# Two attention layers in float32 on one core: projections by seven half-size products, and group-norm averages on VectorE

## The chip, the cores and the metric

The kernel runs on one core of one Trainium2 chip. The metric is the device time of one execution in microseconds; before the change the median of three runs is 4166.9 us (4165.38 to 4168.29).

## The reference, cut to what matters

The input x has 8 images of 32 x 32 positions and 512 channels. Two layers follow each other, each a group norm (32 groups of 16 channels), three projections, attention, and an output projection added onto x:

```
qkv = gn(x) @ w_qkv                          # layer 0: 16 heads of 32
x = x + softmax(q k^T / sqrt(32)) v @ w_proj + b_proj
q, k, v = gn(x) @ Wq, gn(x) @ Wk, gn(x) @ Wv # layer 1: 4 heads of 128
x = x + softmax((q k^T + position logits) / ..) v @ Wo
```

All of it is float32. Per image there are eight products of [1024 x 512] by [512 x 512]: q, k, v and the output projection of each layer.

## The kernel before, in words

Everything is held transposed, channels on partitions: a `block` is [128, 4 chunks, 1024 positions], and eight blocks are in SBUF at a time. PSUM has eight banks: four for the logits of attention 0 (`ps`, one buffer), one for its accumulator (`acc`, one buffer), and three (`bank`) that all else takes in turn.

**Projections.** `project_T` (L210) and `product_T` (L468) make an output [128 channels x 512 positions] in one bank as the sum over four chunks; `project_rows` (L228) makes v with positions on partitions. Each [128 x 128] weight is used as four column tiles of 32 by `by_columns` (L202, matmul at L206). A float32 matmul shows as two instructions in the trace, so one bank is 32 instructions: 4 chunks x 4 column tiles x 2. A projection is 8 banks. `evacuate` (L128, L130) copies a bank to SBUF on ScalarE; the output projections add it onto x on VectorE (L490, L525). Weights come whole, 1 MB, by `load_weight` (L132) on SyncE's queue, two buffers deep.

**Attention 0** (L272) goes by steps of 128 keys. `front` computes logits for 512 queries of four heads (L282) and exponentials on ScalarE (L290, 2048 columns). `back` multiplies by v (L301) and adds up the exponentials on VectorE (`esum`, L310 and L312). After eight steps `hold` copies the accumulator (L262) and `finish` sums `esum` over partitions by matmuls (L321) and calls `normalise` (L265): reciprocal on VectorE (L268), a check of the sums (L249), and a multiplication on GpSimd (L270). **Attention 1** (L382) does the same with 512 columns a step and with the position logits of `position_logits` (L344), whose copies from PSUM alternate between ScalarE (L377) and VectorE (L378).

**Group norm.** `statistics` (L164) takes mean and variance of each channel; `group_norm` (L172) averages over 16 channels by two small matmuls with `gavg` (L176, L186) and normalises in place (L192).

**The order of the work.** The main loop runs b from 0 to 8. In round b the 64 steps of attention 0 of image b go side by side with a list of other work: `after_0` of image b-1 (output projection of layer 0), `after_1` of image b-2 (that of layer 1) with `norm_1` of image b-1 between its parts, `second` of image b-1 (q, k, v of layer 1 with position logits), attention 1 of image b-1 with `load` of image b+1 woven in, and `before_0` of image b+1 (q, k, v of layer 0). `side_by_side` (L548) spreads that list over the steps by the costs that each part yields, one unit being one chunk's matmuls. Attention 1 yields 0, so its 64 steps run together between two steps of attention 0. In round 1 there is no `after_1`, and `norm_1` gets empty cost of 3 x 8 (`ALONE`) in its place:

```
            if past is not None:
                rest.append(woven(after_1(b - 2, past), norm, 1, 1))
                total += PRODUCT
            else:
                rest.append(chain([ALONE], (cost + ALONE for cost in norm)))
                total += 3 * ALONE
```

The tile framework then makes the order on each engine: an instruction that its own plan finds ready may be put ahead of earlier ones that wait. At run time each engine takes its instructions strictly in that order.

Of the kernel before, what the change touches and what calls it, by code (L numbers as in the profile page):

```python
# [9 lines left out]
F32 = mybir.dt.float32  # L10
# [17 lines left out]
def quick_path(  # L28
# [40 lines left out]
    small = ctx.enter_context(tc.tile_pool(name="small", bufs=4))  # L69
# [20 lines left out]
    with nc.allow_non_contiguous_dma(reason="512 values, once"):  # L90
# [6 lines left out]

    ng = P // GROUP_CHANNELS
    gind = consts.tile([P, ng], F32, tag="gind", name="gind")
    nc.vector.tensor_reduce(  # L100
        gind, ident.rearrange("p (g k) -> p g k", k=GROUP_CHANNELS), axis=AX.X, op=ALU.add
    )
    gavg = consts.tile([P, P], F32, tag="gavg", name="gavg")
    nc.vector.tensor_scalar(
        gavg.rearrange("p (g k) -> p g k", k=GROUP_CHANNELS),
        gind.unsqueeze(2).to_broadcast([P, ng, GROUP_CHANNELS]),
        1.0 / GROUP_CHANNELS,
        None,
        op0=ALU.mult,
    )  # L110
# [17 lines left out]
    def evacuate(dst, src):  # L128

        nc.scalar.copy(dst, src)  # L130

    def load_weight(w, col0, name):  # L132
        t = mem.tile([P, CC, NB], F32, tag="w", name=name, bufs=2)
        nc.sync.dma_start(t, w.rearrange("(cc p) n -> p cc n", p=P)[:, :, col0 : col0 + NB])
        return t
# [9 lines left out]
    def fetch(kept, name):  # L145
        xT = chunks(block(name))
        for cc in range(CC):
            nc.sync.dma_start(xT[cc], kept[cc])
        return xT
# [5 lines left out]
    def load_blocks(b, cc):  # L155

        xs = mem.tile([P, N // 32, 32], F32, tag="xs", name=f"xs_{b}_{cc}", bufs=2)
        for a in range(P // 32):
            nc.sync.dma_start(
                xs[32 * a : 32 * a + 32], by_blocks(xf[b], cc * P + 32 * a)  # L160
            )
        return xs.rearrange("p t i -> p (t i)")

    def statistics(st, xT, cc, name):  # L164
        if cc == 0:
            st["mv"] = small.tile([P, CC, 2], F32, tag="mv", name=f"mv_{name}")
        s = small.tile([P, NH, 6], F32, tag="st", name=f"st_{name}_{cc}")
        for h in range(NH):
            nc.vector.bn_stats(s[:, h, :], xT[cc][:, h * NB : (h + 1) * NB])
        nc.vector.bn_aggr(st["mv"][:, cc, :], s.rearrange("p h s -> p (h s)"))  # L170

    def group_norm(st, xT, name):  # L172

        mv = st["mv"]
        pm = bank(f"pm_{name}", [P, CC])
        nc.tensor.matmul(pm, gavg, mv[:, :, 0], start=True, stop=True)  # L176
        mean = small.tile([P, CC], F32, tag="mean", name=f"mean_{name}")
        nc.vector.tensor_copy(mean, pm)

        off = small.tile([P, CC], F32, tag="off", name=f"off_{name}")  # L180
        nc.vector.tensor_sub(off, mv[:, :, 0], mean)
        nc.vector.tensor_mul(off, off, off)
        nc.vector.tensor_add(off, off, mv[:, :, 1])
        yield 0
        pv = bank(f"pv_{name}", [P, CC])
        nc.tensor.matmul(pv, gavg, off, start=True, stop=True)  # L186
        var = small.tile([P, CC], F32, tag="var", name=f"var_{name}")
        nc.vector.tensor_scalar_add(var, pv, GN_EPS)
        rstd = small.tile([P, CC], F32, tag="rstd", name=f"rstd_{name}")
        nc.gpsimd.tensor_tensor(rstd, var, neg_half, op=ALU.pow)  # L190
        for cc in range(CC):
# [10 lines left out]
    def by_columns(out, weights, moving, start, stop):  # L202

        for g in range(P // 32):
            columns = slice(32 * g, 32 * g + 32)
            nc.tensor.matmul(  # L206
                out[columns, :], weights[:, columns], moving, start=start, stop=stop
            )

    def project_T(xn, w, dsts, name):  # L210

        for m in range(CC):
            for h in range(NH):
                pa = bank(f"pa_{name}_{m}_{h}")
                for cc in range(CC):
                    by_columns(
                        pa,
                        w[:, cc, m * P : (m + 1) * P],
                        xn[cc][:, h * NB : (h + 1) * NB],
                        start=(cc == 0),  # L220
                        stop=(cc == CC - 1),
                    )
                    if cc == CC // 2 - 1:
                        yield CC // 2
                evacuate(dsts(m)[:, h * NB : (h + 1) * NB], pa)
                yield CC // 2

    def project_rows(xn, w, y, name):  # L228

        for t in range(NT):  # L230
            pa = bank(f"pa_{name}_{t}")
            for cc in range(CC):
                by_columns(
                    pa,
                    xn[cc][:, t * P : (t + 1) * P],
                    w[:, cc, :],
                    start=(cc == 0),
                    stop=(cc == CC - 1),
                )
                if cc == CC // 2 - 1:  # L240
                    yield CC // 2
            evacuate(y[:, t, :], pa)
            yield CC // 2

    def check_sums(rec, su, name):
        junk = mem.tile([P, NB], F32, tag="junk", name=f"jk_{name}", bufs=1)
# [3 lines left out]
            out=junk,  # L250
# [8 lines left out]

    def hold(acc, name):  # L260
        held = mem.tile([P, NB], F32, tag="held", name=f"hd_{name}", bufs=2)
# [837 lines left out]
```

## Time and profile before

| | |
|---|---|
| median of three runs | 4166.9 us |
| the profiled execution | 4168.86 us |
| its span, first to last instruction | 4167.1 us |
| mean granted TensorE clock | 0.995 |
| busy: TensorE, VectorE, ScalarE, GpSimd | 4068.1, 2295.5, 1663.9, 279.7 us |
| TensorE on the eight projections (L206) | 234 to 243 us each over the 8 images |
| DMA | 172.10 MB, mean 41 GB/s |

In the profile PE is TensorE's matmuls, PEld its weight loads, DVE VectorE, ACT ScalarE, POOL GpSimd and SP the queue of SyncE. A line of a group reads: line, engine, operation, output<-inputs, shapes, count | busy us, mean ns of one | idle us before them and what ended it. The end of a matmul is modelled, and matmuls overlap, so the time between the starts of matmuls says more than a mean duration does.

### The profile page before, as it was taken

Reading aid. Unit: us, or ns where it says so; the run is one execution under the profiler, and the core shown is the slowest. Engines: PE = TensorE matmul, PEld = TensorE weight load, DVE = VectorE, ACT = ScalarE, POOL = GpSimd, SP = SyncE. Lnnn points to the kernel's source line nnn. Section 1 sums busy time; section 2 is a strip of 40 time slices with the busy share of each in tenths; the row PEclk is TensorE's granted clock in tenths of the full one; section 3 lists DMA queues with packets and bytes.
Section 4 is the critical chain, followed back from the end, with each engine's and each line's share of the span. In section 5 each row is a group of like instructions: output and inputs, shape, how many; then the busy total and the mean of one; then the engine's idle time right before and its main releaser. Section 6 shows DMA issues by size and latency. Waiting matters only on the chain.

```text
span 4167.1 us, 64679 instructions
## 1 busy us (share of the span) xinstructions
PE 4068.1 (98%) x28866; PEld 1359.1 (33%) x28866; DVE 2295.5 (55%) x1977; ACT 1663.9 (40%) x1665; POOL 279.7 (7%) x155
## 2 busy tenths in 40 slices
PE   7999999999999999999999999999999999999998
PEld 2222234222442224322243223432234322234343
DVE  2566565464654655546555564655556457555244
ACT  1554543434434343343533435344453444542131
POOL 0000000000010000100000000000000000001000
PEclk9999999999999999999999999999999999999999
DMA  4101020031200302012020120202210022010201
GB/s 122 31 31 41 11 61 0 21 97 37 51 1 24 109 21 51 1 68 65 21 51 11 67 57 21 51 11 72 52 37 25 11 77 46 15 57 2 70 31 22
DMA packets 320896, 172.10 MB, mean 41 GB/s; under 512 B 271424, under 2 KB 271456, under 8 KB 320608
## 3 DMA queue, kind: packets, MB, share of 16 engines
q1 hardware_dynamic: 320512, 167.81, 14.2%
q8 instruction: 228, 3.74, 0.4%
q14 instruction: 60, 0.49, 0.0%
q0 software_dynamic: 96, 0.07, 0.0%
HBM read 117.51 MB, written 50.33 MB: 40 GB/s over the span
## 4 chain that ended last, share of the span: by engine, by line
PE 90%; DVE 6%; ACT 3%; DMA 0%; issue 0%; SPq 0%; POOL 0%; DVEq 0%; ACTq 0%; POOLq 0%
PE ps L282 12%; PE acc L301 11%; PE ps L392 10%; PE pa_q L206 10%; PE pp L206 10%; PE acc L404 10%; PE pa_k L206 9%; PE pa_v L206 9%; PE ps L393 3%; DVE rc L268 2%; ACT e L290 2%; PE su L321 1%; ACT posT L377 1%; PE su L423 1%; DVE es L310 1%; DVE posT L378 1%
## 5 line engine op out<-in xcount | busy, mean ns | idle before, releaser
L290 ACT ACTIVATE e<-ps 128x2048 f32<-128x2048 f32 x512 | 961.5, 1878 | 955.7 <-PE ps L282 789.0
L312 DVE TENSOR_TENSOR es<-es,e 128x2048 f32<-128x2048 f32 x384 | 880.1, 2292 | 701.4 <-ACT e L290 701.4
L282 PE MATMUL ps<-q,k 32*128 32x512 f32 x4096 | 605.9, 644 | 47.5 <-ACT e L290 47.4
L268 DVE RECIPROCAL rc<-su 128x512 f32<-128x512 f32 x128 | 429.8, 3357 | 358.6 <-PE su L321 326.7
L395 ACT ACTIVATE e<-ps 128x512 f32<-128x512 f32 x512 | 305.9, 597 | 709.9 <-PE ps L393 656.9
L301 PE MATMUL acc<-e,v 128*32 128x512 f32 x4096 | 550.4, 610 | 1.0 <-ACT e L290 1.0
L392 PE MATMUL ps<-q,k 128*128 128x512 f32 x1024 | 534.5, 604 | 5.5 <-ACT e L395 5.5
L404 PE MATMUL acc<-e,v 128*128 128x512 f32 x1024 | 522.3, 593 | 0.0
L270 POOL TENSOR_TENSOR q<-hd,rc 128x512 f32<-128x512 f32 x128 | 259.4, 2027 | 3617.9 <-DVE rc L268 3165.6
L415 DVE TENSOR_TENSOR es<-es,e 128x512 f32<-128x512 f32 x384 | 285.8, 744 | 252.1 <-ACT e L395 250.9
L393 PE MATMUL ps<-posT,sel 128*128 128x512 f32 x512 | 406.9, 795 | 0.0
L282 PEld LDWEIGHTS ps<-q,k 32*128 32x128 f32 x4096 | 165.3, 183 | 479.2 <-issue 256.7
L392 PEld LDWEIGHTS ps<-q,k 128*128 128x128 f32 x1024 | 184.3, 189 | 268.7 <-issue 185.2
L206 PE MATMUL pa_v<-wv,x1T 128*32 128x512 f32 x2048 | 243.4, 594 | 0.0
L206 PE MATMUL pa_k<-x1T,wk 128*32 128x512 f32 x2048 | 242.5, 596 | 0.0
L206 PE MATMUL pa_q<-x0T,wq 128*32 128x512 f32 x2048 | 238.0, 599 | 3.5 <-DVE x0T L192 3.5
L404 PEld LDWEIGHTS acc<-e,v 128*128 128x128 f32 x1024 | 192.6, 189 | 145.3 <-issue 103.8
L206 PE MATMUL pp<-q,wo 128*32 128x512 f32 x2048 | 235.6, 592 | 2.9 <-DVE checks L249 2.9
L206 PE MATMUL pa_q<-x1T,wq 128*32 128x512 f32 x2048 | 236.6, 594 | 0.0
L206 PE MATMUL pa_v<-wv,x0T 128*32 128x512 f32 x2048 | 235.8, 592 | 0.0
L206 PE MATMUL pa_k<-x0T,wk 128*32 128x512 f32 x2048 | 235.8, 592 | 0.0
L206 PE MATMUL pp<-q,wp 128*32 128x512 f32 x2048 | 234.4, 592 | 0.0
(67 smaller groups left out, 2276.7 us busy)
## 6 DMA issues: line engine op xcount, KB each, us to landing
xs<-in_x SPq DMA_DIRECT2D x128, 128.0 KB, 3.4
d<-x0T SPq DMA_DIRECT2D x32, 512.0 KB, 3.8
x1T<-d SPq DMA_DIRECT2D x32, 512.0 KB, 5.7
d<-x1T SPq DMA_DIRECT2D x32, 512.0 KB, 2.6
x2T<-d SPq DMA_DIRECT2D x32, 512.0 KB, 7.9
out<-ot SPq DMA_DIRECT2D x256, 64.0 KB, 1.9
wq<-in_L_conv_w_qkv SPq DMA_DIRECT2D x8, 1024.0 KB, 5.2
wk<-in_L_conv_w_qkv SPq DMA_DIRECT2D x8, 1024.0 KB, 5.6
```

The source lines that it names most:

```text
L206: nc.tensor.matmul(out[columns, :], weights[:, columns], moving, start=start, stop=stop)
L268: nc.vector.reciprocal(rec, su)
L270: nc.gpsimd.tensor_tensor(dst, held, rec, op=ALU.mult)
L282: nc.tensor.matmul(ps[:, r, :], k[m][rows, j * P : (j + 1) * P], q[m][rows, h * NB : (h + 1) * NB], start=True, stop=True,)
L290: nc.scalar.activation(e, ps, AF.Exp, scale=D0 ** -0.5)
L301: nc.tensor.matmul(acc[r * D0 : (r + 1) * D0, :], v[:, j, c0 : c0 + D0], e[:, r, :], start=(j == 0), stop=(j == NT - 1),)
L312: nc.vector.tensor_add(state["esum"], state["esum"], e)
L392: nc.tensor.matmul(ps, k[h][:, keys], q[:, h, queries], start=True, stop=False)
L393: nc.tensor.matmul(ps, sel[:, keys], posT[:, h, queries], start=False, stop=True)
L395: nc.scalar.activation(e, ps, AF.Exp, scale=1.0 / math.sqrt(D1))
L404: nc.tensor.matmul(acc, v[:, j, h * D1 : (h + 1) * D1], e, start=(j == 0), stop=(j == NT - 1),)
L415: nc.vector.tensor_add(state["esum"], state["esum"], e)
```

## The change

**Seven products.** The products go by the Winograd form of Strassen's method. The input is cut into halves of channels (two chunks each, `HC`) and of positions (`NB` = 512), the weight into halves of both sides. `forms` makes three sums of quarters of the input in buffers of their own and one in place, four VectorE instructions of 1024 columns. Four sums of quarters of each weight are made once, at the start (`add_up`), and kept in DRAM: for w_qkv on VectorE, for the other five weights on GpSimd and its queue.

`seven` makes a quarter of an output pair, two units `u` a projection. It has three banks x, y and z, and seven products in the order 0, 5, 6, 4, 1, 2, 3, each of two chunks:

```
        x = bank(f"x_{name}")
        product(x, 0, True)
        p1 = snapshot("e1", f"p1_{name}")
        nc.scalar.copy(p1, x)
        yield HC
        y = bank(f"y_{name}")
        product(y, 5, True)
        a = snapshot("es1", f"a_{name}")
        nc.vector.tensor_add(a, y, p1)
        sink.early(p1, a)
        yield HC
        z = bank(f"z_{name}")
        product(z, 6, True)
        p7 = snapshot("e1", f"p7_{name}")
        nc.scalar.copy(p7, z)
        yield HC
        product(y, 4, False)
        b = snapshot("es1", f"b_{name}")
        nc.vector.tensor_add(b, y, p1)
        sink.middle(b, p7)
        yield HC
        product(x, 1, False)
        sink.c11(x)
        yield HC
        product(y, 2, False)
        sink.c12(y, p1)
        if hook is not None:
            hook()
        yield HC
        product(z, 3, False)
        sink.c21(z, a)
        sink.late(p7)
        yield HC
```

So a bank is read after a part of its products, and further products are added to it afterwards. `Plain` (q, k, v) writes the four results with one ScalarE copy (c11), two VectorE additions (c12, c21) and one GpSimd addition (b + p7). `Onto` (output projections) adds onto x with three GpSimd additions (p1, a, b) and four on VectorE. In the row form (v) the weight quarter streams, 256 columns at a time, and each bank is two halves:

```
                for t in range(2):
                    for c in range(HC):
                        by_columns(
                            out[:, t * HN : (t + 1) * HN],
                            f[:, c, (2 * u + t) * P : (2 * u + t + 1) * P],
                            w[c],
                            start and c == 0 and t == 0,
                            c == HC - 1,
                            True,
                        )
```

**Weights** come as quarters of 128 KB by `Stream`, in 16 buffers on SyncE's queue: after a product has used its quarter, the same quarter for the next unit is asked for.

**Group norm.** Mean and variance of the channels are transposed in 32 x 32 blocks on VectorE, summed over 16 channels by `tensor_reduce`, spread, and transposed back; the matmuls with `gavg` are gone:

```
-        pm = bank(f"pm_{name}", [P, CC])
-        nc.tensor.matmul(pm, gavg, mv[:, :, 0], start=True, stop=True)
...
+        nc.vector.transpose(turned, mv)
+        avg = small.tile([P, 2, 32], F32, tag="avg", name=f"avg_{name}")
+        averages(avg[:, 0, :], turned, 0)
...
+        nc.vector.transpose(back.rearrange("p a c -> p (a c)"), avg.rearrange("p a c -> p (a c)"))
```

**Attention's ends.** The accumulator is copied straight into q, the buffer `held` goes. The sums are copied from PSUM to SBUF by ScalarE before the reciprocal reads them, and the sums of attention 0 take the `acc` bank and not one of the three. `finish` of attention 0 moves to the start of the next step.

```
+        su = mem.tile([P, NB], F32, tag="rec", name=f"su_{name}", bufs=2)
+        nc.scalar.copy(su, acc_sums)
+        rec = mem.tile([P, NB], F32, tag="rec", name=f"rc_{name}", bufs=2)
+        nc.vector.reciprocal(rec, su)
...
-        nc.gpsimd.tensor_tensor(dst, held, rec, op=ALU.mult)
+        nc.gpsimd.tensor_tensor(dst, dst, rec, op=ALU.mult)
```

**The order.** `after_1` of image b-2 now comes first in a round, then `after_0` of image b-1, and `norm_1` stands alone, with its three times 8 of empty cost, in every round that has attention 0. `forms` of the next part is called as a hook in the last unit of the part before, after its sixth product; that of `norm_1`'s result stands at the start of `second`. The last round keeps `norm_1` woven into `after_1`. Position logits are woven in after the first product of each of the four units of k and v. x is loaded in pieces of half the size.

```
+                if past is not None:
+                    rest.append(after_1(b - 2, past, forms_0))
+                    total += PRODUCT
+                rest.append(later(after_0, b - 1, last))
                 rest.append(chain([ALONE], (cost + ALONE for cost in norm)))
-                total += 3 * ALONE
+                total += PRODUCT + 3 * ALONE
```

## The prediction

> **What bounds the kernel now.** I read first the page's busy shares and the chain that ended last.
>
> ```profile
> PE 4068.1 (98%) x28866; PEld 1359.1 (33%) x28866; DVE 2295.5 (55%) x1977; ACT 1663.9 (40%) x1665; POOL 279.7 (7%) x155
> ...
> PE 90%; DVE 6%; ACT 3%; DMA 0%; issue 0%; SPq 0%; POOL 0%; DVEq 0%; ACTq 0%; POOLq 0%
> ```
>
> The span is TensorE's (PE): 98% busy and 90% of the chain. An average hides stages, so I took one steady period (1417.0 to 1924.6 us, from one batch's norm to the next's) in three windows: attention 0 beside projections, attention 1 alone, attention 0 beside projections.
>
> ```profile
> 1417.00:1594.50 177.50, 174.57 (x1587) 51.49 (x1579) 99.41 (x78) 84.17 (x72) 11.87 (x5) 1.00 0.12 29
> 1594.50:1727.00 132.50, 131.60 (x340) 61.75 (x337) 81.66 (x101) 41.92 (x71) 11.42 (x8) 1.00 0.17 40
> 1727.00:1924.60 197.60, 197.60 (x1695) 54.88 (x1693) 104.02 (x69) 81.78 (x66) 13.58 (x6) 1.00 0.16 56
> ```
>
> Columns: length, then PE, PEld, DVE, ACT, POOL busy, clock, DMA share. PE is full in all three; VectorE (DVE) has 203.4 of 375.1 us beside attention 0, that is 54%. So PE time taken out comes off the span, as long as nobody else makes PE wait.
>
> **Seven products for eight.** The last product of the kernel runs undisturbed and gives its price (PE's timeline):
>
> ```profile
> 4124.96 27.67 PE L206 MATMUL pp<-q,wo 128*32 128x512 f32 x256
> 4152.57 0.38 PE L614 MATMUL pf<-bad,ones 128*128 128x1 f32 x2
> ```
>
> From start to start 27.61 us for 256 instructions: 64 sets of four column tiles, 0.431 us a set. There are 8 projections in 8 batches, 64 x 27.61 = 1767 us, and the change issues 7/8 of the columns: **-221 us**.
>
> Of these, the two row projections (v of each layer) now stream 256 columns and not 512: 2 projections x 14 products x 8 sets x 8 batches = 1792 sets of half the width. No row has that width; two widths beside it, from the tile view of pp:
>
> ```profile
> L206 PE MATMUL pp<-q,wo x2048: 589/592/617, 897.3 to 4152.0; 128*32 128x512 f32 x187
> L365 PE MATMUL pp<-q,ph_sb x512: 272/273/299, 489.4 to 3984.0; 128*32 128x128 f32 x171
> ```
>
> (592 - 273)/384 = 0.831 ns a column, 425 ns of the set's 431; 6 ns are fixed, so a half set takes 219 where half of 431 is 215.5. 1792 x 3 ns = **+5 us**. Bounds: 0 (no fixed part), and +44 if a set can't come faster than the mixed sets of pp do (32 instructions from 1508.12 to 1510.04, 240 ns a set). I take 5, from the row of the same shape.
>
> [...]
>
> **Group norm off PE.** Each norm's two small matmuls moved PE's stream by 0.31 us each (starts 1415.04 to 1415.35 and 1421.63 to 1421.94): 16 norms x 0.62 = **-10 us**. Some ten tiny DVE instructions (0.1 to 0.2 us in this trace) replace five and two round trips.
>
> Floor so far, from the profiled run's own 4168.9 (span 4167.1, 2.0 above the median): 4168.9 - 221 + 5 - 10 = **3943**.
>
> **What DVE, ScalarE (ACT) and POOL get.** Prices:
>
> ```profile
> L312 DVE TENSOR_TENSOR es<-es,e 128x2048 f32<-128x2048 f32 x384 | 880.1, 2292 | 701.4 <-ACT e L290 701.4
> L268 DVE RECIPROCAL rc<-su 128x512 f32<-128x512 f32 x128 | 429.8, 3357 | 358.6 <-PE su L321 326.7
> L525 DVE TENSOR_TENSOR x2T<-pp,x2T 128x512 f32<-128x512 f32 x64 | 44.1, 689 | 52.7 <-PE pp L206 52.7
> L130 ACT COPY k<-pa_k 128x512 f32<-128x512 f32 x128 | 75.1, 586 | 186.7 <-PE pa_k L206 186.5
> L270 POOL TENSOR_TENSOR q<-hd,rc 128x512 f32<-128x512 f32 x128 | 259.4, 2027 | 3617.9 <-DVE rc L268 3165.6
> ```
>
> - forms: four DVE sums of 1024 columns; between 0.69 (512) and 2.29 (2048) that is 1.22 each, 4.9 a call, 32 calls: 157 us.
> - 96 units that write q, k, v: four DVE adds of 0.69 (265 us), three ACT copies for four (-56), one POOL add of 2.0 (195).
> - 32 units of the two output projections: two DVE adds more (45), two ACT copies more (38), three POOL adds (195).
> - The sums' copy out of PSUM: 128 x 0.59 = 75 on ACT.
>
> DVE becomes 2295 + 467 + some 16 for norms = 2778 us, 70% of the span; ACT 1721, POOL some 700. None is the bound as a total. Beside attention 0, DVE gets 203.4 + 12 x 2.76 + 4 x 1.4 + 3 x 4.9 = 257 us of some 346 (375.1 - 27.6 - 1.2): 74%. So the extra work is hidden, but DVE now stands in PE's way: x, y and z of a unit hold all three banks, and PE may not go on adding to a sum before DVE has read it. What this adds:
>
> - **Two tight reads a unit** (y for a, y for b), with one product of 1.72 us (4 x 0.431) between. The read takes 0.69, so PE waits if DVE is over 1.03 us late. DVE is busy 74% with pieces of 2.29: mean excess 1.26²/(2 x 2.29) x 0.74 = 0.26 us; an attention step also covers 64 of 112 gaps, leaving 0.11. 16 units x 2 x 8 batches = 256 reads: **+28** (0 where the planner fills every gap; 85 at 0.33).
> - **forms in a hook** (ao0, ao1, 16 times): 4.9 us against two products, 3.4, and sometimes a step: **+8** (0 to 24).
> - **Norm 1 alone.** Before, after_1 ran beside it, except in the first round, where the trace shows what a lone norm costs (PE):
>
> ```profile
> 408.36 0.39 PE L176 MATMUL pm<-mv,gavg 128*128 128x4 f32 x2
> 408.68 1.14 PE L282 MATMUL ps<-q,k 32*128 32x512 f32 x8
> 409.75 1.06 PE L301 MATMUL acc<-e,v 128*32 128x512 f32 x8
> 413.80 0.59 PE L186 MATMUL pv<-off,gavg 128*128 128x4 f32 x2 [2.99 <-DVE off L183]
> 414.32 2.09 PE L282 MATMUL ps<-q,k 32*128 32x512 f32 x8
> 416.34 1.94 PE L301 MATMUL acc<-e,v 128*32 128x512 f32 x8
> 418.05 1.87 PE L206 MATMUL pa_q<-x1T,wq 128*32 128x512 f32 x8
> ```
>
> 9.7 us for 4.5 of work (two steps of 1.96 and 0.6): 5.2 lost, part of it a step at half speed after the gap. Now seven rounds have it; the PE round trips go, but s1 and s2 come in front of the second product. I take 7.2 each: 7 x 7.2 - 5.2 = **+45** (9 at 2 each, 79 at 12).
> - **Position logits** want a fourth bank. Their copies form a serial chain of 7 us (ACT 1510.37 to DVE 1517.39), which two banks of products covered; now z waits for that bank. 32 times 0.7: **+22** (0 where the five products that need no z go first, 45 at 1.4).
> - **Start.** The first 24.5 us move 200 GB/s with the DMA engines 92% busy. 1 MB of weights goes ahead of x on SP (5.2 us), s1 and s2 take 2.4, POOL's queue fetches more weights at the same time (8): **+16** (8 to 30).
> - **End.** The last product needed only the first half of its input; forms needs all: copy 0.6, reciprocal 3.4, POOL 1.3 and two sums 2.4 against 3.4 of products, and a slow clock: **+6** (0 to 10).
> - **SP's queue.** 896 loads of 128 KB in place of 64 of 1 MB: at some 0.4 us of issue 360 us of a 4000 us queue; 1 MB landed in 5 to 7 us, and each is asked for a unit, 12 us, ahead. Priced at nothing; if that cover is gone, a unit waits some 3 us.
>
> Sum: 3943 + 28 + 8 + 45 + 22 + 16 + 6 = **4068 us**, 2.4% less.
>
> [...]
>
> **Rivals.**
> - *PE stays as full as before* (3965 to 4000): the planner moves other matmuls into every gap, as it does now (gaps of 0.6 to 1.2 us, a few a period). Only start, end and the norms remain: 3943 + 16 + 6 + 20 = 3985. Against it: all banks taken. Chance 0.22.
> - *DVE costs more than I took*, norms at 12 us and reads at 0.25: 4068 + 34 + 36 = 4138 (4130 to 4158). Chance 0.10.
> - *DVE paces PE, slower*: reads queue behind reciprocal, check and attention sum (3.36 + 0.76 + 2.29). 256 reads at w us each: 4040 + 256w crosses 4167 at w = 0.50; at 1.0 it gives 4296. For it: 74% busy with pieces up to 3.4 us. Against it: the half of gaps that a step covers. Chance 0.13; as much as no change 0.03.
> - *A half-wide matmul costs like a full one*, so that the row products double: 1792 x 0.212 = 380 more, 4448. L365 speaks against it. Chance 0.02.
>
> **Numbers.** Forecast 4068 (4000 to 4130), chance 0.50. Faster 0.50 + 0.22 + 0.10 = 0.82, same 0.03, slower 0.15, where 0.2% is about what measurement can tell from no change. Range 3965 to 4195: all low ends together give 3955, all high ends 4255; below nothing the added waits can't go, but the new order could drop old ones, at most the 47.5 us that the page has as idle before L282. About 0.16 is left out, most of it above.
>
> **What would show it.** PE's projections at 7/8, half sets starting 0.22 us apart; DVE near 70%, POOL near 17%; PE waits named after DVE's reads of open sums below 30 us; gaps of some 7 us with a halved clock at each norm 1. I am wrong if PE waits on DVE in each unit, if half sets start over 0.24 apart, or if weights arrive late.

## The result, and the profile after

The changed kernel takes 4296.65 us (median of four runs, 4289.69 to 4299.51) beside 4166.34 for the kernel before in the same rounds: a ratio of 1.031, 95% interval 1.029 to 1.033. It is 3.1% slower, where 2.4% faster was forecast (4068, range 3965 to 4195). The profiled execution took 4289.69 us, its span 4287.9.

The page of the changed kernel, busy shares and the chain that ended last, against the same two lines of before (PE 98%, PE 90% of the chain):

```profile
PE 3933.5 (92%) x30338; PEld 1429.0 (33%) x30338; DVE 2840.1 (66%) x2659; ACT 1719.9 (40%) x1761; POOL 576.6 (13%) x393
...
PE 73%; DVE 15%; ACT 4%; issue 3%; POOL 1%; DMA 0%; another core or an unknown queue 0%; SPq 0%; DVEq 0%; ACTq 0%; POOLq 0%
```

TensorE is busy 135 us less, but stands in 8% of the span, and VectorE has 15% of the chain where it had 6%. The reader sees already that no engine is full: what grew is waiting. Where, the windows of one steady round tell (length, then PE, PEld, DVE, ACT, POOL busy, clock, DMA share; the round, its first 220 us, the rest):

```profile
1990.00:2505.40 515.40, 485.98 (x3800) 176.32 (x3796) 352.65 (x331) 214.78 (x220) 66.01 (x44) 0.98 0.20 54
1990.00:2210.00 220.00, 191.83 (x1824) 61.56 (x1820) 145.20 (x129) 94.95 (x82) 29.71 (x19) 0.96 0.20 53
2210.00:2505.40 295.40, 294.15 (x1981) 114.76 (x1976) 207.45 (x203) 119.83 (x138) 36.30 (x26) 1.00 0.20 55
```

This is the most telling view of the case. After 2210 us, with layer 0's projections for the next image beside attention 1 and attention 0, TensorE is full at full clock. All waits lie in the first 220 us: 28.2 us of standing, and a clock of 0.96. There stand the lone norm, layer 1's q, k, v and the position logits.

The round closes as an account. Before, the windows of its round held 174.57 + 131.60 + 197.60 = 503.8 us of work in 507.6. The seven products should take 27.6 off it and the norms 1.2: 475. After, 486.0 us are busy. The records show five stretches of 3.41 us at half clock in this round, all before 2210; TensorE streamed during 15.5 us of them, and half of that, 7.8, is lost: 478 us of work at full clock. **So TensorE's work fell nearly as forecast**, 3 us short of it; 29.4 us of standing (3.8 before) and 8 of slow clock came on top, and the round went from 507.7 to 515.4.

TensorE's timeline at three places of that stretch (start, length, engine, line, what; in brackets the idle time before and what ended it):

```profile
2033.23 1.07 PE L517 MATMUL acc<-e,v 128*32 128x512 f32 x8
2039.58 1.92 PE L294 MATMUL x_q<-x1T,w_q 128*32 128x512 f32 x2 [5.28 <-DVE x1T L280]
...
2088.23 1.04 PE L294 MATMUL y_q<-f_xn,w_q 128*32 128x512 f32 x8
2091.86 1.14 PE L498 MATMUL ps<-q,k 32*128 32x512 f32 x8 [2.58 <-ACT e L506]
...
2110.62 1.04 PE L517 MATMUL acc<-e,v 128*32 128x512 f32 x2
2115.07 3.33 PE L294 MATMUL z_k<-x1T,w_k 128*32 128x512 f32 x16 [3.40 <-issue]
```

The first is the lone norm. The second is an attention end: the banks of the scores (`ps`) are free only when a late exponential has read them. The third is z, which needs the bank that the position logits hold; its 16 matmuls then take 3.33 us from start to end, where 16 at full clock take 1.92 (`x_wo` at 4240.51). "issue" names nobody; the rows of ScalarE and VectorE show what the second and the third waited for:

```profile
2089.93 1.88 ACT L506 ACTIVATE e<-ps 128x2048 f32<-128x2048 f32 x1 [5.21 <-DVE es L526]
...
2107.96 1.10 ACT L593 CAST posT<-pp 32x512 fp32r<-32x512 f32 x1 [1.46 <-PE pp L581]
2109.10 1.01 DVE L594 TENSOR_TENSOR posT<-pp,posT 32x512 fp32r<-32x512 f32 x1 [1.69 <-ACT posT L593]
...
2113.66 0.58 ACT L593 CAST posT<-pp 32x512 fp32r<-32x512 f32 x1 [1.07 <-DVE posT L594]
2114.26 1.88 ACT L506 ACTIVATE e<-ps 128x2048 f32<-128x2048 f32 x1
2114.27 0.69 DVE L594 TENSOR_TENSOR posT<-pp,posT 32x512 fp32r<-32x512 f32 x1 [0.65 <-ACT posT L593]
```

The exponential of 2089.93 had waited for the first attention sum (`es<-e,e`), which stood on VectorE behind the reciprocal (from 2082.46), the check and the sum a_q. The copies of the logits alternate between the two engines, each waiting for the other, and end at 2114.96; z starts at 2115.07. The groups of TensorE's rows over the whole kernel (busy, mean ns, then idle before and its releasers) add this up:

```profile
L498 PE MATMUL ps<-q,k 32*128 32x512 f32 x4096 | 616.1, 653 | 87.3 <-ACT e L506 87.1
L294 PE MATMUL x_q<-x1T,w_q 128*32 128x512 f32 x512 | 97.6, 620 | 42.7 <-DVE x1T L280 36.3 <-DMA w_q<-in_L_conv_Wq 6.5
L294 PE MATMUL y_q<-f_xn,w_qkv 128*32 128x512 f32 x768 | 96.9, 603 | 10.5 <-DVE b_q L361 10.5
L294 PE MATMUL y_wp<-f_ao,w_p 128*32 128x512 f32 x768 | 93.9, 602 | 10.0 <-DVE b_wp L361 5.7 <-DVE f_ao L312 4.3
L294 PE MATMUL z_v<-w_v,x1T 128*32 128x256 f32 x1024 | 83.5, 479 | 54.1 <-DVE posT L594 29.8 <-issue 24.3
L294 PE MATMUL z_k<-x1T,w_k 128*32 128x512 f32 x512 | 83.1, 736 | 51.2 <-DVE posT L594 30.8 <-issue 20.4
L294 PE MATMUL x_q<-x0T,w_qkv 128*32 128x512 f32 x512 | 66.5, 623 | 51.4 <-DMA w_qkv<-in_L_conv_w_qkv 45.8 <-DVE x0T L280 5.6
```

The scores' row of the kernel before:

```profile
L282 PE MATMUL ps<-q,k 32*128 32x512 f32 x4096 | 605.9, 644 | 47.5 <-ACT e L290 47.4
```

Logits' bank (z_k and z_v of layer 1) 105.3 us, scores 87.3 (before 47.5), the lone norm 36.3, the start 51.4 (45.8 of it until the first product), and all rows of y together 39.0, of which 26.0 are for VectorE's sums a and b. The last number matters for the rivals: y is the open sum, the bank that VectorE reads before TensorE has added all its products to it.

### The profile page after: what moved, and what is told of

Same layout as the page of the kernel before. It is cut to its first block, busy times and chain, and to the rows that moved or that the text cites. A ratio compares the mean times of both kernels' runs of the same rounds, so it can differ in the third digit from the quotient of the medians.

```text
span 4287.9 us, 71270 instructions
## 1 busy us (share of the span) xinstructions
PE 3933.5 (92%) x30338; PEld 1429.0 (33%) x30338; DVE 2840.1 (66%) x2659; ACT 1719.9 (40%) x1761; POOL 576.6 (13%) x393
## 4 chain that ended last, share of the span: by engine, by line
PE 73%; DVE 15%; ACT 4%; issue 3%; POOL 1%; DMA 0%; another core or an unknown queue 0%; SPq 0%; DVEq 0%; ACTq 0%; POOLq 0%
PE acc L620 10%; PE ps L608 10%; PE ps L498 10%; PE acc L517 8%; DVE rc L473 4%; DVE es L526 3%; PE y_q L294 3%; PE y_k L294 3%; PE z_k L294 3%; PE y_v L294 3%; PE ps L609 3%; PE x_q L294 3%; PE z_v L294 3%; PE x_k L294 2%; ACT e L506 2%
## 5 line engine op out<-in xcount | busy, mean ns | idle before, releaser
L498 PE MATMUL ps<-q,k 32*128 32x512 f32 x4096 | 616.1, 653 | 87.3 <-ACT e L506 87.1
L486 POOL TENSOR_TENSOR q<-q,rc 128x512 f32<-128x512 f32 x128 | 210.7, 1646 | 1702.2 <-DVE rc L473 1660.9
L631 DVE TENSOR_TENSOR es<-es,e 128x512 f32<-128x512 f32 x384 | 260.3, 678 | 130.7 <-ACT e L611 120.3
L517 PEld LDWEIGHTS acc<-e,v 128*32 128x32 f32 x4096 | 85.4, 109 | 395.5 <-issue 346.8
L526 DVE TENSOR_TENSOR es<-e,e 128x2048 f32<-128x2048 f32 x64 | 193.5, 3024 | 16.2 <-ACT e L506 16.2
L594 DVE TENSOR_TENSOR posT<-pp,posT 32x512 fp32r<-32x512 f32 x128 | 110.1, 860 | 135.9 <-ACT posT L593 134.9
L476 DVE CUSTOM_DVE_ANT_0 su<-su,rc 128x512 f32<-128x512 f32 x128 | 158.5, 1238 | 2.0
L593 ACT CAST posT<-pp 32x512 fp32r<-32x512 f32 x128 | 104.3, 815 | 135.7 <-DVE posT L594 93.8
L609 PEld LDWEIGHTS ps<-posT,sel 128*128 128x128 f32 x512 | 97.3, 190 | 122.5 <-issue 122.5
L471 ACT COPY su<-sums 128x512 f32<-128x512 f32 x128 | 75.1, 586 | 155.2 <-PE sums L538 82.6
L294 PE MATMUL y_q<-f_xn,w_q 128*32 128x512 f32 x768 | 133.3, 605 | 4.3 <-DVE f_xn L312 4.3
```

The costliest lines, as they stand in the source:

```text
L294: nc.tensor.matmul(out[columns, :], weights[:, columns], moving, start=start, stop=stop, skip_group_check=open_sum,)
L498: nc.tensor.matmul(ps[:, r, :], k[m][rows, j * P : (j + 1) * P], q[m][rows, h * NB : (h + 1) * NB], start=True, stop=True,)
L517: nc.tensor.matmul(acc[r * D0 : (r + 1) * D0, :], v[:, j, c0 : c0 + D0], e[:, r, :], start=(j == 0), stop=(j == NT - 1),)
L526: nc.vector.tensor_add(state["esum"], state["first"], e)
L609: nc.tensor.matmul(ps, sel[:, keys], posT[:, h, queries], start=False, stop=True)
L631: nc.vector.tensor_add(state["esum"], state["esum"], e)
```

## The experiments

In the table, "round" is a steady round's length, "idle" the sum of the gaps between TensorE's matmuls after the first one, "half" the time that the records show at half clock. All but the ratio come from the profiled execution of each; "half" counts in every kernel a last stretch that lies mostly behind TensorE's last matmul (10 to 14 us). e5, e9, e12, e13 and e14 leave a part of the calculation out, as said below.

| kernel | us | ratio to before, 95% | round | idle | half |
|---|---|---|---|---|---|
| before | 4166 | 1 | 507.7 | 66 | 46 |
| changed | 4297 | 1.031 (1.029-1.033) | 515.4 | 295 | 237 |
| e1 logits later | 4206 | 1.010 (1.008-1.012) | 505.2 | 238 | 172 |
| e2 casts first | 4269 | 1.025 (1.023-1.027) | 511.7 | 275 | 210 |
| e3 norm beside | 4345 | 1.043 (1.042-1.045) | 525.6 | 343 | 312 |
| e4 light start | 4286 | 1.029 (1.028-1.031) | 515.4 | 290 | 244 |
| e5 cheap reciprocal | 4155 | 0.998 (0.997-0.999) | 501.7 | 200 | 144 |
| e6 before + ends | 4156 | 0.998 (0.997-0.999) | 502.1 | 75 | 59 |
| e7 before + group norm | 4134 | 0.992 (0.990-0.994) | 502.5 | 54 | 38 |
| e8 e1 + e2 + e4, check late | 4159 | 0.998 (0.997-0.999) | 498.0 | 205 | 162 |
| e9 before, cheap reciprocal | 4115 | 0.988 (0.986-0.989) | 502.5 | 45 | 29 |
| e10 before + norm + ends | 4160 | 0.999 (0.998-1.000) | 502.7 | 80 | 65 |
| e11 product on VectorE | 4294 | 1.031 (1.029-1.033) | 518.4 | 275 | 267 |
| e12 e8, cheap reciprocal | 4055 | 0.974 (0.972-0.975) | 489.7 | 121 | 98 |
| e13 open sums not read | 4279 | 1.028 (1.026-1.029) | 518.1 | 275 | 277 |
| e14 no early sums | 4250 | 1.020 (1.018-1.022) | 508.7 | 272 | 213 |
| e15 reciprocal in pieces | 4277 | 1.027 (1.025-1.029) | 515.4 | 279 | 244 |
| e16 e8, in pieces | 4165 | 1.000 (0.999-1.000) | 498.0 | 203 | 151 |
| e17 seven: qkv 0 and output 1 | 4135 | 0.994 (0.993-0.995) | 498.2 | 130 | 107 |
| e18 seven: qkv 0 alone | 4111 | 0.987 (0.986-0.989) | 495.4 | 92 | 74 |

My theory after the result: the seven products save nearly what was forecast, and the order around them (a bank that the logits hold, a norm with nothing beside it, exponentials that come late) gives more than that back, most of it in one stretch. The rival is the prediction's own: VectorE paces TensorE at every reading of an open sum; its formula gave 4296 at 1.0 us a reading, which is the measured time.

**e1 and e2: the logits' bank.** e1 weaves the logits in four products later, so that four products, and not one, stand before the next that needs their bank; e2 lets ScalarE's four casts go ahead of VectorE's four sums.

```
-  yield from woven(keys_and_values, position_logits(q, posT, b), 0, len(ORDER))
+  yield from woven(keys_and_values, position_logits(q, posT, b), 4, len(ORDER))
```

```
     nc.scalar.copy(view[rows], pp[rows])
-    nc.vector.tensor_sub(view[rests], pp[rows], view[rows].bitcast(F32))
+    parts.append((view, rows, rests))
+ for view, rows, rests in parts:
+    nc.vector.tensor_sub(view[rests], pp[rows], view[rows].bitcast(F32))
```

> The changed kernel, with the position logits woven in after the fifth product of each unit of k and v in place of the first: their bank is then taken when x's bank is free, and four products, not one, stand between them and the next product that needs a bank. Theory 1 (the fourth bank: z waits 3.4 to 4.9 us for the bank of the logits four times a round, and PE goes on at half clock after it): the 124 us of waits ahead of z_k and z_v go, and some 50 us of half clock with them, so about 4130 us, and no round has z waiting on posT. Rival (VectorE is simply too full, 66% over the span, and holds PE wherever it can): the same VectorE work is there, so the waits move elsewhere and the time stays within 30 us of 4297.

> The changed kernel, with the four ScalarE copies of a logits tile issued first and the four VectorE subtractions after them, so that the copies no longer wait for a subtraction each. Theory 1: the bank is held some 4.5 us in place of 7, so 32 waits get 2 to 2.5 us shorter, about 4220 us. Rival (VectorE too full): nothing is taken off VectorE, so within 20 us of 4297.

Measured -90 and -28 us, each between its two cases; in e2 z still waits 91.4 us for the bank. e1's rows for z and the scores:

```profile
L498 PE MATMUL ps<-q,k 32*128 32x512 f32 x4096 | 621.9, 658 | 114.9 <-ACT e L506 114.7
...
L294 PE MATMUL z_k<-x1T,w_k 128*32 128x512 f32 x512 | 71.0, 592 | 0.5 <-DVE posT L594 0.5
L294 PE MATMUL z_v<-w_v,x1T 128*32 128x256 f32 x1024 | 68.8, 379 | 0.9 <-DVE posT L594 0.9
```

The wait for the bank is gone (105.3 to 1.4), and part of it turned up at the scores (87.3 to 114.9); all standing fell by 57 us, and the time that TensorE streamed at half clock by 67 (184 to 117); with half of the latter, that is the 90. One place in the order was the largest single wait, and moving it was half a repair: VectorE was late for the next thing.

**e3: the norm beside the output projection again.** Before's order, `after_0`, then `after_1` woven with the norm.

> The changed kernel with the order of before: the output projection of layer 0 first, then that of layer 1 with norm 1 beside it in every round that has one, no empty cost after the first round. Theory (a lone norm costs PE 5.9 us and a stretch at half clock, 48.6 us of waits ahead of x_q in all): about 60 us less, 4235 us. Rival: the norm's some 10 us on VectorE (averages, four normalisations, the sums of forms) then hold up the reads of the output projection that runs beside it, and the time stays within 20 us.

It went the other way, +49. The idle time ahead of x_q, where the norm stands, shrank (42.7 to 16.6), but two others came:

```profile
L294 PE MATMUL y_wo<-f_ao,w_o 128*32 128x512 f32 x768 | 106.3, 653 | 58.5 <-DVE a_wo L351 51.6 <-DVE f_ao L312 4.4 <-DVE b_wo L361 2.4
L294 PE MATMUL y_wp<-f_ao,w_p 128*32 128x512 f32 x768 | 104.1, 659 | 36.2 <-DVE f_ao L312 36.2
```

y_wp now waits for its forms, for which the new order had a place and this one has none, and y_wo for a sum that VectorE queues behind the norm. So the products need the new order or another place for their forms, and this run is no clean test of the norm's price.

**e4: a light start.** The sums of the weights that are needed late are made after the first projections.

> The changed kernel with the first unit's weight quarters asked for right after the sums of the first weight, ahead of x, and with the sums of the five other weights on GpSimd placed behind the first projections. Theory (the first product waits until 45.8 us for 128 KB that stand in the queue behind 4 MB, and b_q at 67.8 us waits 9 us for GpSimd, which is busy with those sums): first product near 34 us and no wait near 68, about 4275 us. Rival (x itself is what takes the time, with the DMA engines 76% busy over the first 132 us): 5 us at most.

-11, half of what was expected; the first product comes at 38 us, not 34.

**e5 and e9: a cheap reciprocal, in the changed kernel and in the one before.**

```
-  nc.vector.reciprocal(rec, su)
+  nc.vector.tensor_copy(rec, su)
```

> The changed kernel with the reciprocal of the sums left out: a copy of the sums stands in its place, so attention outputs are multiplied by the sums and not divided. It takes some 3 us off VectorE 128 times, 390 us of its 2840. Theory 1 (waits of z for the bank of the logits, lone norms, the start): these do not depend on the reciprocal, and only the 45 us go that attention 0's waits for exponentials grew by, with some half clock: 4230 to 4260 us. Rival (VectorE too full as a whole): every read of an open sum comes sooner, 4130 us or less.

> The kernel before with its 128 reciprocals replaced by copies, so that the attention outputs are multiplied by the sum and not by its reciprocal: the control for the same edit in the changed kernel, which took 142 us off. Theory (the time of VectorE's pieces matters in the changed kernel because three banks of open sums leave TensorE nothing to do while it is late; before, TensorE had other work): little, 4120 to 4165 us, since the page of before has only 47.5 us idle ahead of the scores (L282). Rival (the reciprocal costs the same before and after, so the 142 us tell nothing of the change): 3995 to 4055.

-142 and -50; both leave the division out. The control falls just below the first of my two cases (4115 for 4120 to 4165): even where TensorE was 98% busy, VectorE's time had a price, 50 us for 335 us less of it (0.15); after the change 142 for 399 (0.36). The scores' waits of e5:

```profile
L498 PE MATMUL ps<-q,k 32*128 32x512 f32 x4096 | 603.6, 646 | 26.3 <-ACT e L506 26.1
```

From 87.3 to 26.3, and the halved clock from 237 to 144 us. ScalarE's idle time that ended with the first attention sum fell from 214 us to 67: exponentials wait for that sum, and it stands behind the reciprocal on VectorE.

**e6, e7 and e10: parts of the change without the products.** The kernel before with the new attention ends, with the group norm on VectorE, and with both.

> The kernel before, with the new ends of attention alone: accumulator copied straight into q, sums copied to SBUF by ScalarE ahead of the reciprocal, sums of attention 0 in the accumulator's bank, finish of attention 0 at the start of the next step. Theory 3 (the new ends lengthen the chain sums, copy 0.7, reciprocal 3.4, check 0.7 to 1.2, attention sum 3.0, next exponential, by some 2.5 us in 64 places, and part of that reaches PE): 4185 to 4210 us. Rival (the ends are free, and the waits come from the products' units): within 8 us of 4166.

> The kernel before, with group norm's averages on VectorE alone. PE's stream loses 64 small matmuls, 0.31 us each for two, so 4156 us by the prediction's term of 10 us. Rival (the eleven small VectorE instructions hold up what runs beside them): 4166 or more.

> The kernel before with two parts of the change, the group norm's averages on VectorE and the attention's new ends, and without the seven products. Alone they gave -32.5 and -10.5 us. If each takes away its own waits: 4123 (4118 to 4130). If both relieve the same waits of TensorE: 4130 to 4140. Either way faster than both kernels, and the seven products with their order and start then cost the difference to 4297, some 165 to 175 us, where the prediction had them at -221 and +119.

-10, -32 and -5. The group norm alone gives three times the 10 us of the prediction, and e7 beats both kernels. The ends alone cost no time, against my expectation; together the two give no more than the ends alone and far less than the norm, against both cases expected. Each takes the same 5 us off a round (502.1, 502.5, 502.7). Why the ends then lose what the norm gains outside the steady rounds stays open. But the ends alone bring scores that wait longer: 63.9 us in e6, and in e10

```profile
L283 PE MATMUL ps<-q,k 32*128 32x512 f32 x4096 | 596.0, 648 | 71.4 <-ACT e L291 71.2
```

So 24 of the 40 us by which this wait grew are there without any of the seven products. With norm and ends in place, the products with their order cost 4297 - 4160 = 137 us.

**e8 and e12: repairs together.** e8 is e1, e2 and e4, and the check of attention 0's sums four steps later; e12 the cheap reciprocal on top.

> The changed kernel with the logits after the fifth product, the logits' copies ahead of the subtractions, the light start, and the check of attention 0's sums put off to the fourth step after. If the causes are apart and add up: 4297 - 91 - 11 and, with the bank's wait gone already, some 5 for the copies and 20 to 40 for the check (0.7 to 1.2 us earlier, 64 times, and a VectorE sum that no longer runs beside GpSimd's product), 4150 to 4170 us. If the check's place does not matter: 4185 to 4190 us.

> The changed kernel with the logits' copies first and woven later, the light start and the check deferred (4159 us together), and the reciprocal replaced by a copy (attention outputs are multiplied by the sum and not by its reciprocal). Theory (the seven products do save TensorE some 216 us, and only waits and the halved clock behind them gave it back): the waits ahead of the scores fall from 114 to about 40 us and the halved clock with them, 4020 to 4060 us. Rival (the late exponentials were already relieved by the other edits, or something else than waits is lost): 4110 to 4150.

-138, and a further -104: 4055. Idle falls to 121 us, half clock to 98, and nothing of the seven products was touched. But e12 leaves the division out, and its fair neighbour is e9, which does the same to the kernel before: 4115. Against that, 60 us are won with the waits gone; without these repairs e5 loses 40 to e9. With the division in, e8 only draws level with e10 (4159 and 4160).

**e11: does GpSimd slow VectorE?** The product at each attention end goes to VectorE.

```
-  nc.gpsimd.tensor_tensor(dst, dst, rec, op=ALU.mult)
+  nc.vector.tensor_tensor(dst, dst, rec, op=ALU.mult)
```

> The changed kernel with the product at each attention end (output times reciprocal) on VectorE and not on GpSimd. Theory (a GpSimd sum or product beside VectorE slows VectorE: first attention sum 2.23 to 3.35 us, check 0.68 to 1.24 us): VectorE gets 128 x 0.69 = 88 us more and loses 128 x (1.12 + 0.56) = 215 us; by the reciprocal's 2.75 us an end for 142 us, 1.0 us an end is some -50, so 4230 to 4265, with the first sum back near 2.23. Rival (the slower sums are not due to GpSimd, or nobody waits for them): 4290 to 4340, for VectorE only has more to do.

The mechanism is as expected, the first attention sum and the check get short again (3024 and 1238 ns in the changed kernel):

```profile
L526 DVE TENSOR_TENSOR es<-e,e 128x2048 f32<-128x2048 f32 x64 | 147.5, 2305 | 9.6 <-ACT e L506 9.6
...
L476 DVE CUSTOM_DVE_ANT_0 su<-su,rc 128x512 f32<-128x512 f32 x128 | 91.4, 714 | 2.1
```

but the time isn't: 4294 for 4297. My sum was wrong (64 first sums, not 128), and with the product VectorE's total falls by 29 us only. The scores' wait falls (87.3 to 73.7) while the halved clock grows (237 to 267). The contention of the two engines is real here and has no price that shows.

**e13 and e14: the rival, taken away.** e13 leaves out the reading at the same number of VectorE sums; e14 leaves out the sums too. Both leave a part of the products out of the result.

```
-  nc.vector.tensor_add(a, y, p1)
+  nc.vector.tensor_sub(a, p1, p1)
...
-  nc.vector.tensor_add(b, y, p1)
+  nc.vector.tensor_sub(b, p1, p1)
```

> The changed kernel with its two early readings of the open sum y left out: a and b are p1 - p1 (zero) and not y + p1, the same number of VectorE sums of the same size, on tiles that are long ready, so that TensorE may go on adding to y at once. The projections are wrong by what y held. Theory (the open sums cost little: gaps ahead of products into y add up to some 39 us, with their share of the halved clock): 40 to 65 us less, 4230 to 4257. Rival (VectorE paces TensorE at 256 readings of 1.0 us each, as the prediction's slower case had it): 4030 to 4090.

> The changed kernel without those two sums at all (p1 takes the place of a and b): the waits on y go as in the run before, and 128 x 2 = 256 VectorE sums of 0.69 us, 177 us of its time, with them. The projections are wrong by what y held. If the load of VectorE is what makes exponentials and copies late (theory): by the cheap reciprocal's 142 us for 373 us of VectorE time another 50 to 70 us below the run without readings, 4165 to 4205. If load doesn't matter: within 15 us of that run.

-18, and a further -29 (less than I expected, for 210 us less of VectorE's time: 0.14). The rival asked for over 200. Without any reading of an open sum the kernel stays 2.8% slower than before, so **the rival that named the measured time had the wrong mechanism**; the match was an accident. My own price was too high too. One thing isn't equal: VectorE is busy 49 us longer in e13 (2889 for 2840), which by the prices here (0.14 to 0.36) hides 7 to 18 us of the gain. In e13's rows nothing of a or b is left; y waits 14.0 us for forms, 7.9 for a weight and 3.2 for another sum of VectorE. Two of the rows:

```profile
L294 PE MATMUL y_q<-f_xn,w_qkv 128*32 128x512 f32 x768 | 96.5, 598 | 0.0
...
L294 PE MATMUL y_wp<-f_ao,w_p 128*32 128x512 f32 x768 | 93.7, 601 | 4.3 <-DVE f_ao L312 4.3
```

**e15 and e16: the length of VectorE's pieces.** Attention 0's reciprocals in four pieces of 128 columns over four steps, in the changed kernel and on top of e8.

```
+  def piece(at):
+      cols = slice(at * P, (at + 1) * P)
+      nc.vector.reciprocal(rec[:, cols], su[:, cols])
...
+  late += [lambda i=i: piece(i) for i in range(NB // P)] + [last]
```

> The changed kernel with attention 0's reciprocals cut into four pieces of 128 columns, one behind each of the next four steps, then the product and the check; the same work, nothing left out. If what hurts is the length of the piece in front of the attention sums (VectorE 3.4 us away while TensorE's scores wait for the exponential): most of the 92 us by which the cheap reciprocal gained more here than in the kernel before, 4190 to 4240. If it is VectorE's load: 4280 to 4300.

> The same reciprocal in pieces on top of the kernel with logits' copies first and woven later, light start and check deferred (4159 us); nothing left out. If the piece's length hurts: 4085 to 4125, a version faster than the kernel before, than the group norm alone (4134) and than the change. If load: 4140 to 4160.

-20 and nothing. So the length of one piece counts for little; this theory of mine fell. Next to e5, that leaves the amount of VectorE's work at the attention ends, which was not tested by itself.

**e17 and e18: seven products only where TensorE was full.** If the waits belong to one stretch, products should pay outside it. e17 keeps seven in layer 0's q, k, v and layer 1's output projection and takes eight plain ones elsewhere, with the norm beside the output projection as before and a light start; e18 also makes that output projection plain. From e18's edit:

```
- WP, WQ1, WK1 = Matrix(w_proj, 0, "p"), Matrix(Wq, 0, "q1"), Matrix(Wk, 0, "k1")
- WV1, WO = Matrix(Wv, 0, "v1"), Matrix(Wo, 0, "o")
+ WP, WQ1, WK1 = Matrix(w_proj, 0, "p", True), Matrix(Wq, 0, "q1", True), Matrix(Wk, 0, "k1", True)
+ WV1, WO = Matrix(Wv, 0, "v1", True), Matrix(Wo, 0, "o", True)
...
+ for n in range(2):
+     for h in range(NH):
+         out = bank(f"o{n}{h}_{name}")
+         for k in range(2):
+             w = stream.take(QUARTERS[2 * n + k])
+             for c in range(HC):
+                 by_columns(out, w[c], x[:, k * HC + c, h * NB : (h + 1) * NB], k == 0 and c == 0, k == 1 and c == HC - 1)
...
```

> A kernel with seven products only where TensorE kept its cover in the changed kernel's steady round (q, k, v of layer 0 and the output projection of layer 1), and eight plain products for the output projection of layer 0 and q, k, v of layer 1, the stretch in which all of a round's long waits lay (lone norm, position logits, late exponentials). The norm stands beside layer 1's output projection again; group norm and attention ends as changed; light start. Nothing is left out. Theory (the seven products pay where other work is at hand, and cost what they cost through waits in that one stretch): from the run with group norm and ends alone, 4160 us, 4/8 of the 221 us off (-110), start +10, some 240 us more VectorE time at 0.13 to 0.17 us each +36, open sums +5: 4100 (4060 to 4135), below every kernel so far that leaves nothing out. Rival (seven products load VectorE and the banks so much that they lose wherever they are): 4160 to 4230.

> As the run with seven products in layer 0's q, k, v and layer 1's output projection (4135 us), with that output projection back to eight plain products; nothing is left out. There TensorE waited 27 us ahead of y of the output projection, 22.6 of them for VectorE's reading a, behind the norm that stands beside it; q, k, v of layer 0 waited 1 us. Theory (the products lose where VectorE has a norm or a chain of copies to do at the same time, and pay beside plain attention): +27.6 for the eighth products, -27 for those waits, -10 for the halved clock behind them, -18 for VectorE (forms and sums), -4 at the start: 4105 (4090 to 4130). Rival (the waits only move to the next place, and VectorE's load costs wherever it is): 4135 to 4165.

4135 and 4111. e17 kept only 25 of the 110 us that it should save against e10; its rows named the place, a reading queued behind the norm:

```profile
L298 PE MATMUL y_wo<-f_ao,w_o 128*32 128x512 f32 x768 | 104.8, 656 | 27.1 <-DVE a_wo L355 22.6 <-DVE f_ao L316 4.6
...
L298 PE MATMUL y_q<-f_xn,w_qkv 128*32 128x512 f32 x768 | 96.9, 593 | 1.1 <-DVE f_xn L316 1.1
```

Three projections with seven products win more than four with them: e18 is 1.3% faster than before, the fastest kernel that leaves nothing out. Not all of that is the products': the group norm alone gives 32 of these 55 us. e18 is 22 us below e7 and 49 below e10, where three projections ask for 83. The windows of its steady round, to be held against those of the changed kernel:

```profile
1862.20:2357.50 495.30, 491.29 (x3989) 180.85 (x3985) 320.30 (x287) 213.47 (x218) 37.00 (x26) 1.00 0.18 48
1862.20:2082.20 220.00, 216.33 (x2076) 67.23 (x2076) 138.89 (x110) 98.64 (x79) 9.94 (x7) 0.99 0.21 54
2082.20:2357.50 275.30, 274.96 (x1919) 113.61 (x1915) 181.41 (x178) 114.83 (x139) 27.06 (x19) 1.00 0.15 44
```

503.8 less 3/8 of 27.6 and the norms' 1.2 asks for 492.2 us; 491.3 are busy, 1.7 of them lost to half clock. 4 us of waits are left.

## Why the prediction was wrong, point by point

- **Seven products for eight (-221) and half-wide sets (+5): right, nearly.** A steady round's work fell to 478 us where the sum asks for 475, and e18's to 490 where 492 is asked. The half-wide tiles take 379 ns where the full ones take 592, and the sets follow each other 0.216 us apart (z_v of layer 1: 1178.14, 1178.36, 1178.57), the four starts of a set within 20 ns (1178.14 to 1178.16).
- **Group norm (-10): right in sign, too small.** -32 alone: TensorE stands 12 us less and is busy 28 less, and its first matmul comes 6 later. What the part beyond the small matmuls is due to wasn't tested.
- **Two tight reads (+28): right in kind.** The rows of y stand 26.0 us for a and b; e13 took 18 off.
- **Forms (+8):** 13.0 us, in three waits, one of them (4.4) at the end. **Lone norm (+45):** 36.3 us of standing, with a slow clock behind it (half clock for 3.41 us from 2039.5 in the round shown). **Start (+16):** the first product 21.3 us later than the first projection of before, and 9.3 of standing behind it (also in the 26.0), just above its bounds (8 to 30). **End (+6):** 5.2 us of standing and a slow clock (half for 6.83 us from 4247.9). **SP's queue (0):** one row of layer 1's x waits 6.5 us for a weight.
- **Position logits (+22): the term that failed by size.** The bank cost 105.3 us of standing, and e1 gave 90 us of time back. I took 0.7 us for each of 32 cases; they cost 3.3 on average. The chain of copies was as long as I took it: 6.9 to 7.2 us in 24 of the 32 cases (11.7 to 11.9 in the other eight, behind a reciprocal). What failed is the cover: at 0.7 us a case I took nine tenths of the chain as covered by other work, but in the case shown y's product and one attention step were all that stood before z, and z waited 3.1 to 4.3 us in 28 cases. Only in the last round, without attention 0, was it 0 to 0.5.
- **Late exponentials: no term.** The prediction had VectorE at 74% beside attention 0 and "None is the bound as a total", and concluded that the extra work is hidden apart from the reads; the new attention ends got no price but a copy on ScalarE. The scores' waits went from 47.5 to 87.3 us, 24 of the 40 by the ends and the norm alone (e10), and e9, e14 and e5 show VectorE's time at 0.14 to 0.36 us per us, before the change already. This is the step that failed in principle: 74% is an average, and the exponentials that TensorE needs wait for one sum behind the reciprocal.
- **The halved clock: no term of its own.** It went from 46 us to 237, and the work streamed in it from 33 to 184 us, so that some 76 us were lost, a third of the difference between 4068 and the result. I gave it to the norm, the end and no other place, though it came behind gaps of 2.5 us and more all along the kernel, in 49 stretches.

In sum, on the profiled runs: 4168.9 - 221 + 5 - 10 = 3943; 229 us more standing (idle 66 to 295), 27 before TensorE's first matmul (19.2 to 45.8) and 76 of slow clock give 4275, 15 us short of the 4289.7 of that run.

- **The rivals.** "VectorE paces TensorE, slower" had the sign and even 4296, by 256 readings of 1.0 us. Its readings cost some 18 to 36 us in all (e13, and e13 with VectorE's 49 us priced). So the match was luck: neither the forecast's mechanism nor the rival's was it.

What isn't settled: how much of the +137 that the products cost over e10 goes to each of bank, norm and load, for the repairs overlap (e1, e2 and e4 alone make 129, together with the late check 138; the cheap reciprocal makes 142 alone and 104 on top of them). The norm's place wasn't tested cleanly.

## What to carry to other kernels

Before work is taken out of a full engine, ask of each stretch what that engine does while its helpers are late; the helper's average share doesn't tell. An algorithm with fewer multiplications holds more banks open and has more readers: use it in the stretches where the windows show a full engine, and leave it out where a norm or a chain of copies runs (beside e10, which has the same norm and ends, three projections of eight won 1.2%, all eight lost 3.3%). And when a rival names the measured number, take its mechanism away before believing it.

## What the hardware showed that was not expected

**The clock falls after short waits.** The changed kernel has 49 stretches at half clock before TensorE's last matmul, 34 of them of 3.4 us, the others of 6.8 or 10.2; the largest gap in the ten us before each is 2.5 to 9.3 us, in 16 cases under 3.4 and in 5 under 3.0 (the ends of matmuls are modelled). In the kernel before it is 1.7 to 3.0 us for all eight. How long a wait has to be for the clock to fall, no run shows.

**VectorE beside GpSimd: who starts first.** A first attention sum takes 3.35 us (median) in the changed kernel, where 2.28 is usual with GpSimd at rest, and e11 brings that back (2.31 on average, in place of 3.02). The kernel before had the same meeting mostly without this delay (2.35 on average). One case of before, then one of after:

```profile
1415.08 2.23 DVE L310 TENSOR_TENSOR es<-e,e 128x2048 f32<-128x2048 f32 x1
1415.31 3.13 POOL L270 TENSOR_TENSOR q<-hd,rc 128x512 f32<-128x512 f32 x1 [50.29 <-DVE rc L268]
...
2209.46 1.78 POOL L486 TENSOR_TENSOR q<-q,rc 128x512 f32<-128x512 f32 x1 [4.53 <-DVE rc L473]
2210.03 3.36 DVE L526 TENSOR_TENSOR es<-e,e 128x2048 f32<-128x2048 f32 x1
```

Of the 55 first sums of before that run beside GpSimd, 45 start ahead of its product and take 2.2 to 2.3 us, and the product takes 2.8 to 3.3 where the shortest take 1.3; in the other ten the product starts first, and the sum takes 2.9. After, the check stands between reciprocal and sum, GpSimd starts first in 51 cases, and the sums take 2.8 to 3.4. So in both kernels the later of sum and product is the one that takes longer; why, no run shows. The check differs between them: before, with one operand in PSUM, it took 0.7 us even where GpSimd had started first (96 cases); after, with both in SBUF, it takes 0.8 to 1.8 there (75 cases). Whether the operand's place makes that difference was not tested by itself.
